# One attention + feed-forward block on one Trainium2 core: the feed-forward put into attention's hand order and buffers

## The chip, the cores and the metric

The kernel runs on one core of a Trainium2 chip. A core has five engines that run their own instruction streams and wait for one another by semaphores: PE (TensorE, matrix products and transposes into the PSUM memory), ACT (ScalarE), DVE (VectorE), POOL (GpSimd) and SP (SyncE, which here only issues transfers). PE's row is split in the profile into the matmuls (PE) and the loads of their stationary operand (PEld). The metric is the device time of one execution in microseconds. Before the change it is 5400.07 us, the median of 3 runs (5399.82 to 5401.36).

## What is computed

`x` is 8 x 1024 x 512 in float32 (B, S, E). The reference, cut to what matters:

```python
def attn(x):                      # H = 16 heads of HD = 32, q and k split into two halves
    q, k, v = split(x @ w_qkv)
    a = softmax(q1 k1 / sqrt(HD)) - lam * softmax(q2 k2 / sqrt(HD))
    out = a @ v
    out_n = out / sqrt(mean(out**2) + 1e-6) * norm_w * (1 - 0.8)
    return rearranged(out_n) @ wo

def ffn(x):                       # hidden 2048, rank 16
    h = bitlinear(x, w_fc) + gate * (x @ v.T @ fast_b.T @ u.T)
    r = maximum(h, 0)
    return bitlinear(r * r, w_proj)

x = x + attn(layernorm(x))
x = x + ffn(layernorm(x))
```

`bitlinear` multiplies by weights rounded to -1, 0 or 1 and by one scale for each output row.

## The kernel before

`block_kernel` runs two phases one after the other: `attention_phase` (lines 25 to 550) and `ffn_phase` (lines 778 to 969). What they share passes through the tensors `x1_dram[0]` to `x1_dram[15]` in DRAM: the rows after attention, in 16 groups of four tiles of 128 rows.

**Attention** works in 256 units: one head of one batch and one half of its queries, 32 units a batch. A unit takes the maxima of the scores (`max_scores`, L201, reduced by DVE at L208), makes the exponentials (`exp_scores`: PE at L254, ACT at L258), adds them up on POOL (`add_up`, L268 and L270) and multiplies by the values (`values`, through `quarters`, L275). `sums` adds the exponentials over the partitions with a matrix of ones (also L275). `heads_out` turns the result (L309) and divides (L319 to L332). After every fourth unit four steps follow: `rms_squares` (ACT, L343), `rms_sums` (DVE, L347), `rms_apply` (POOL, L353 to L356) and `output_rows`, which loads a tile of `x` (L365), multiplies by `wo` on PE (L368), adds (L375) and stores a tile to `x1_dram` (L376).

The order of PE, ACT, DVE and POOL is that in which the program names the instructions (`manual_schedule`); the order of SP's transfers is left to the compiler's scheduler. The loop (L485) makes the maxima two units ahead. The list `fill` holds the preparation of the next batch (layer norm, turning, values, projections: `prepare`), of which one step is taken at the head of a unit, at times also in its middle. In the last batch `fill` is empty, and the feed-forward weights are fetched instead (`prep.fetch`, L492): both halves of `wfc` and the first half of `wpr`. The second half of `wpr` takes the buffer of the last batch's values and is fetched after the loop (`prep.fetch_rest`, L543). Then `sums`, `heads_out` and the four steps of the last tile are written one after the other (L545 to L550), outside of the hand order.

**PSUM** has eight banks: three for `mx` (maxima), four for `one` (everything short) and one for `acc` (values). The feed-forward phase has four for `y`, two for `pf` and two for `tr` and `pt`.

**Feed-forward** takes the 16 groups of 512 tokens one after the other, each in 16 blocks of 128 hidden rows. `hidden(g, j)` makes eight matmuls (L885; tokens are split into a high and a low part, `hTh` and `hTl`) and one with the low-rank term (L888, operands `us` and `ts`); ACT takes the positive part (L890), POOL squares it (L892), DVE splits it into `r2h` and `r2l` (L895, L896). `contract` multiplies the block of two steps before by `wpr` into four banks (L902). At the group's end `output` scales (L913), adds `x` (L919) and stores (L922).

Between the blocks of group g the tokens of group g+1 are prepared: `load` in block 6 (L824, one transfer of 1 MB), `stats` in 7 and 8 (L833 to L838), `center` in 9 to 12 (L844, into `h`, two buffers), `turn` in 10 to 13 (L853 on PE into `tr`; L813 on ACT, L814 on DVE), `low_rank` in 14 (L865 with `m1`; L871 to L875 make `ts`). For group 0 all of it stands ahead of the first block, in the order of the scheduler:

```python
    load(0)
    for i in range(4):
        stats(0, i)
    for i in range(4):
        center(0, i)
        turn(0, i)
    low_rank(0)
```

Of the kernel before, what the change touches and what calls it, by code (L numbers as in the profile page):

```python
# [17 lines left out]
P = 128  # L18
# [6 lines left out]
def attention_phase(  # L25
    ctx, tc, consts, x, w_qkv, wo, lq1, lq2, lk1, lk2, norm_w, x1_dram, dpool, big, prep,
):

# [36 lines left out]
    wv = wpool.tile([P, KC, E], F32, name="wv")  # L65
# [46 lines left out]
    def norm_stats(b, t, xs=None):  # L112
        if xs is None:
            xs = p_x.tile([P, E], F32, tag="x", name="xs")
        nc.sync.dma_start(xs, x[b, t * P : (t + 1) * P])
# [165 lines left out]
    def values(u, kc):  # L281
        b, h = divmod(u // 2, H)
        if kc == 0:
            acc_of[u] = ps_acc.tile([P, HS // 2], F32, tag="acc", name="acc")
        quarters(
            acc_of[u], v_of[b][:, kc, h * HD : (h + 1) * HD], e_of[u, kc // 2][:, kc % 2],
            kc == 0, kc == NS - 1,
        )
# [71 lines left out]
    def output_rows(n):  # L360
# [5 lines left out]
        py = one_bank()  # L366
# [17 lines left out]
    def prepare(b):  # L384
        stats, tiles = {}, {}

        def start():
            begin_batch(b)
            stats[0] = norm_stats(b, 0)

        def advance(t):
# [3 lines left out]
            if t + 3 < NS:  # L395
                stats[t + 3] = norm_stats(b, t + 3)
# [28 lines left out]
    with tc.tile_pool(name="a_stage", bufs=1) as stage, tc.manual_schedule(engines=engines):  # L425
        begin_batch(0)
        xs4 = stage.tile([P, 4, E], F32, tag="tp", name="xs4", bufs=1)
        stats = [norm_stats(0, t, xs4[:, t - 4, :] if t >= 4 else None) for t in range(NS)]
# [44 lines left out]
    p_e = ctx.enter_context(tc.tile_pool(name="a_e", bufs=5))  # L473
    p_es = ctx.enter_context(tc.tile_pool(name="a_es", bufs=2))
    p_o = ctx.enter_context(tc.tile_pool(name="a_o", bufs=2))
    p_y = ctx.enter_context(tc.tile_pool(name="a_y", bufs=1))
    fill, later = [], {}
# [6 lines left out]
    with tc.manual_schedule(engines=engines):  # L484
        for s in range(0, NS * NU + 2, 2):  # L485
# [13 lines left out]
            if u < NU:  # L499
                if u % (2 * H) == 0 and kc == 0:  # L500
                    assert not fill
                    fill = prepare(u // (2 * H) + 1) if u + 2 * H < NU else []
# [40 lines left out]
    prep.fetch_rest()  # L543
    assert not later and list(adds.values()) == list(outs.values()) == [[NU - 1]]
    n = NU // 4 - 1  # L545
    for step in (
        lambda: sums(NU - 1), lambda: heads_out(NU - 1), lambda: rms_squares(n),
        lambda: rms_sums(n), lambda: rms_apply(n), lambda: output_rows(n),
    ):
        whole(step)  # L550
# [227 lines left out]
def ffn_phase(ctx, tc, consts, x1_dram, weights, out):  # L778

    nc = tc.nc
    B, S, E = out.shape
    HID, R = weights.HID, weights.R
    KC = E // P
    NJ = HID // P
    ident, neg_half = consts
    s_fc, s_pr = weights.s_fc, weights.s_pr  # L790


    p_o = ctx.enter_context(tc.tile_pool(name="f_o", bufs=6))
    late = ctx.enter_context(tc.tile_pool(name="f_late", bufs=1))
    early = ctx.enter_context(tc.tile_pool(name="f_early", bufs=1))
    ts = [p.tile([P, 512], F32R, name=f"ts{i}") for i, p in enumerate((early, late))]
    m1 = early.tile([P, KC, P], F32R, name="m1")
    us = early.tile([P, HID], F32R, name="us")
    p_s = ctx.enter_context(tc.tile_pool(name="f_s", bufs=2))
    p_h = ctx.enter_context(tc.tile_pool(name="f_h", bufs=2))  # L800
    nc.sync.dma_start(m1.bitcast(F32), weights.m1_d.rearrange("p k i r -> p k (i r)"))
    nc.sync.dma_start(us.bitcast(F32), weights.us_d)

    ps_y = ctx.enter_context(tc.tile_pool(name="f_ps_y", bufs=4, space=PSUM))
    ps_f = ctx.enter_context(tc.tile_pool(name="f_ps_f", bufs=2, space=PSUM))
    ps_t = ctx.enter_context(tc.tile_pool(name="f_ps_t", bufs=2, space=PSUM))

    p_hT = ctx.enter_context(tc.tile_pool(name="f_hT", bufs=2))
    p_r = ctx.enter_context(tc.tile_pool(name="f_r", bufs=3))

    def split(hi, lo, src):

# [209 lines left out]
```

## Time and profile before

| | us |
|---|---|
| median of 3 runs (lowest to highest) | 5400.07 (5399.82 to 5401.36) |
| the profiled execution | 5402.91 |
| its span, first to last instruction | 5401.1 |
| PE busy | 5293.1 |
| POOL busy | 4125.8 |
| DVE busy | 3791.5 |
| ACT busy | 2829.7 |
| first matmul of the feed-forward's low-rank product | at 4296.6 |

The page of a profile gives each engine's busy time and share. A table of stretches gives for each stretch of time its length, the busy time and number of instructions of each engine (PE, PEld, DVE, ACT, POOL), the granted clock of PE as a share of full speed, the busy share of the DMA engines and what they moved in GB/s. A line of the timeline begins with start and duration in us, then engine, line, operation, output and inputs; in brackets stands how long the engine had been idle before it and which instruction released it. "SPq" marks a transfer issued by SP; its duration is that of the issue. A line of the waits says who waited for whom: total us, how often, the longest.

### The profile page before, as it was taken

To read this page: it belongs to the slowest core of one execution; us is meant where nothing else is said; L and a number is where in the kernel's file an instruction comes from. 1 tells how busy PE (TensorE), PEld (TensorE's weight loads), DVE (VectorE), ACT (ScalarE), POOL (GpSimd) and SP (SyncE) were. 2 spreads that over 40 slices of the span, in tenths; PEclk is the share of its full clock that TensorE was granted. 3 is DMA by queue.
4 is the path that set the end of the run, shared out by engine and by line. 5 is a ranking of instruction groups with operands and counts; after the bars stand their busy time and mean duration, and the time that the engine had idled before them with its cause. 6 is when DMAs were issued, how large, how long until landed. Compare 5 with 4: busy or idle time off the path is not lost.

```text
span 5401.1 us, 105815 instructions
## 1 busy us (share of the span) xinstructions
PE 5293.1 (98%) x41522; PEld 3255.3 (60%) x41522; DVE 3791.5 (70%) x7539; ACT 2829.7 (52%) x5434; POOL 4125.8 (76%) x1501
## 2 busy tenths in 40 slices
PE   8999999999999999999999999999999899999999
PEld 4555555555555555555555555555555577777777
DVE  6877777787778777777787778777888445545554
ACT  4665666566656665665566556655666422222221
POOL 0998899889989998999899889988988633333333
PEclk9999999999999999999999999999999999999999
DMA  8112211211122112111211221122211101111111
GB/s 272 49 51 76 68 55 53 76 65 53 55 76 66 52 59 76 58 57 61 79 53 55 67 76 52 46 68 100 71 46 47 54 19 31 30 31 32 32 32 32
DMA packets 184865, 328.51 MB, mean 61 GB/s; under 512 B 32928, under 2 KB 55456, under 8 KB 183728
## 3 DMA queue, kind: packets, MB, share of 16 engines
q1 hardware_dynamic: 183440, 319.12, 18.5%
q8 instruction: 329, 5.39, 0.4%
q0 software_dynamic: 544, 2.10, 0.1%
q14 instruction: 168, 1.38, 0.1%
q10 hardware_dynamic: 384, 0.52, 0.0%
HBM read 209.16 MB, written 112.46 MB: 60 GB/s over the span
## 4 chain that ended last, share of the span: by engine, by line
PE 75%; POOL 10%; issue 8%; ACT 2%; DVE 2%; DMA 1%; SPq 0%; POOLq 0%; DVEq 0%; ACTq 0%
PE acc L275 17%; PE one L254 15%; PE mx L201 13%; PE one L154 8%; PE one L275 5%; PE one L368 4%; PE one L142 4%; POOL es L270 4%; PE y L902 3%; PE pf L885 3%; ACT e L258 2%; POOL r L892 2%; PE one L309 2%; POOL es L268 2%; POOL o L919 1%
## 5 line engine op out<-in xcount | busy, mean ns | idle before, releaser
L208 DVE TENSOR_REDUCE nm<-mx 128x1 f32<-128x512 f32 x4096 | 2549.4, 682 | 268.1 <-PE mx L201 263.6
L258 ACT ACTIVATE e<-one 128x512 f32<-128x512 f32 x4096 | 2116.9, 603 | 851.2 <-PE one L254 813.3
L270 POOL TENSOR_TENSOR es<-es,e 128x2048 f32<-128x2048 f32 x495 | 2262.4, 4570 | 66.2 <-ACT e L258 34.3
L268 POOL TENSOR_TENSOR es<-e 128x2048 f32<-128x2048 f32 x256 | 1170.0, 4570 | 287.3 <-ACT e L258 287.3
L275 PE MATMUL acc<-e,v 128*32 128x256 f32 x16384 | 1092.1, 384 | 0.0
L201 PE MATMUL mx<-tk,tq 64*128 64x512 f32 x4096 | 1055.8, 469 | 3.0 <-DVE nm L208 2.0
L201 PEld LDWEIGHTS mx<-tk,tq 64*128 64x128 f32 x4096 | 567.1, 183 | 539.8 <-DVE nm L208 303.0
L254 PE MATMUL one<-nms,one 64*128 64x512 f32 x4096 | 831.4, 394 | 8.0 <-ACT e L258 7.5
L254 PE MATMUL one<-tq,tk 64*128 64x512 f32 x4096 | 828.6, 391 | 0.0
L892 POOL TENSOR_TENSOR r<-r 128x512 f32<-128x512 f32 x256 | 270.1, 1058 | 652.8 <-ACT r L890 641.5
L275 PEld LDWEIGHTS acc<-e,v 128*32 128x32 f32 x16384 | 451.5, 109 | 432.0 <-issue 168.8
L890 ACT ACTIVATE r<-pf,s_fc 128x512 f32<-128x512 f32 x256 | 176.5, 690 | 811.0 <-PE pf L888 811.0
L895 DVE CAST r2h<-r 128x512 fp32r<-128x512 f32 x256 | 185.4, 724 | 456.7 <-POOL r L892 454.3
L154 PE MATMUL one<-hT,wqk 128*128 128x512 f32 x1024 | 472.8, 604 | 0.4 <-ACT e L258 0.4
L254 PEld LDWEIGHTS one<-nms,one 64*128 64x128 f32 x4096 | 413.5, 185 | 71.1 <-ACT e L258 15.5
L254 PEld LDWEIGHTS one<-tq,tk 64*128 64x128 f32 x4096 | 396.0, 184 | 82.1
L902 PE MATMUL y<-wpr,r2h 128*128 128x512 f32 x1024 | 415.1, 405 | 0.3
L902 PE MATMUL y<-wpr,r2l 128*128 128x512 f32 x1024 | 403.6, 394 | 0.3 <-DVE r2l L896 0.3
L885 PE MATMUL pf<-hTh,wfc 128*128 128x512 f32 x1024 | 403.5, 394 | 0.0
L885 PE MATMUL pf<-hTl,wfc 128*128 128x512 f32 x1024 | 403.3, 394 | 0.0
L162 DVE SCALAR_TENSOR_TENSOR pc<-one,pc 128x512 fp32r<-128x512 f32 x128 | 88.5, 691 | 345.1 <-ACT pc L161 345.0
L154 PEld LDWEIGHTS one<-hT,wqk 128*128 128x128 f32 x1024 | 184.1, 189 | 214.8 <-issue 186.4
(127 smaller groups left out, 4681.6 us busy)
## 6 DMA issues: line engine op xcount, KB each, us to landing
qk<-pc SPq DMA_DIRECT2D x128, 512.0 KB
tk<-qk SPq DMA_DIRECT2D x256, 256.0 KB
tq<-qk SPq DMA_DIRECT2D x512, 128.0 KB
xs<-in_L_attn_x SPq DMA_DIRECT2D x64, 256.0 KB
xr<-in_L_attn_x SPq DMA_DIRECT2D x256, 64.0 KB
x_dram<-y SPq DMA_DIRECT2D x64, 256.0 KB
xs<-x_dram SPq DMA_DIRECT2D x16, 1024.0 KB
out<-o SPq DMA_DIRECT2D x248, 64.0 KB
```

The source lines that it names most:

```text
L142: nc.tensor.matmul(pv, hT_of[b][:, kc, c * P : (c + 1) * P], wv[:, kc, :], start=(kc == 0), stop=(kc == KC - 1),)
L154: nc.tensor.matmul(ps, wqk[:, kc, c0 : c0 + P], hT_of[b][:, kc, tok], start=(kc == 0), stop=(kc == KC - 1),)
L201: nc.tensor.matmul(mx[sm], tq_of[u][rows, c * P : (c + 1) * P], tk_of[u // 2][rows, kh * 512 : kh * 512 + 512], start=True, stop=True,)
L208: nc.vector.tensor_reduce(nm_of[u][:, kh, sm, c : c + 1], mx[sm], AX.X, ALU.max, negate=True)
L254: nc.tensor.matmul(st[sm], w[rows, cols], m[rows, :], start=(w is one2), stop=(w is not one2))
L258: nc.scalar.activation(e[:, kc % 2, sm, :], st[sm], AF.Exp)
L268: nc.gpsimd.tensor_add(es_of[u], e_of[u, 0], e)
L270: nc.gpsimd.tensor_add(es_of[u], es_of[u], e)
L275: nc.tensor.matmul(out[32 * g : 32 * g + 32, :], w, e[:, g // 2, (g % 2) * (HS // 2) : (g % 2 + 1) * (HS // 2)], start=start, stop=stop,)
L885: nc.tensor.matmul(pf, w[:, kc, :], hT[:, kc, :], start=(kc == 0 and i == 0), stop=False)
L892: nc.gpsimd.tensor_mul(r2, r, r)
L902: nc.tensor.matmul(ys[i], r2[:, i * P : (i + 1) * P], weights.wpr[j // (NJ // 2)][:, j % (NJ // 2), :], start=(j == 0 and k == 0), stop=(j ...
```

## The change

Both phases become one function, `block_phases`, with the hand order over all of it from the attention loop on. In its parts:

- While the last batch runs, `fill` holds six steps of `prepare_tokens`: the four tiles of token group 0 are loaded, normed, turned and split. They take buffers of attention that are free by then (`pc`, `wv`, `x`).
- The pools of the exponentials (`a_e`, `a_es`) close after the loop, with `fetch_rest` and the last `sums` inside. Pools of the feed-forward (`us`, `m1`, `ts`, then tokens and outputs) open in their place; `m1` and `us` are loaded there.
- The last tile's `heads_out`, `rms_squares`, `rms_sums`, `rms_apply` and `output_rows` are written into blocks 0, 1, 2, 3 and 5 of group 0, with `low_rank(0)` ahead of block 0.
- The feed-forward uses attention's PSUM banks and buffers: `pf` in the three `mx` banks, `y` in the four `one` banks, `tr` and `pt` in the single `acc` bank; the squared values in `tq` and `tk`, tokens of even groups in `x`, `pc` and `wv`. The square is made in place.
- `h` has one buffer instead of two. The split of a turned tile is two instructions on ACT and two on DVE instead of one and one. Even groups are loaded by four transfers of 256 KB.
- `center`, `turn` and `low_rank` come one block later (10 to 13, 11 to 14, 15).

The diff, cut to its core:

```diff
+    p_h = ctx.enter_context(tc.tile_pool(name="a_h", bufs=1))
+    def begin_tokens(g):
+        if g % 2 == 0:
+            his = [p_pc.tile([P, 2, HS], F32R, tag="pc", name="hTh") for _ in range(2)]
+            lo = wpool.tile([P, KC, 512], F32R, tag="wv", name="hTl")
+        else:
+            hi = f_x.tile([P, KC, 512], F32R, tag="hTh", name="hTh")
+            his = [hi[:, 0:2], hi[:, 2:4]]
+            lo = f_x.tile([P, KC, 512], F32R, tag="hTl", name="hTl")
...
+    def split_turned(parts, i, tr):
+        his, lo = parts
+        cols = slice(i * P, (i + 1) * P)
+        for k in range(2):
+            nc.scalar.copy(his[k][:, :, cols], tr[:, 2 * k : 2 * k + 2, :])
+        for k in range(2):
+            nc.vector.tensor_sub(
+                lo[:, 2 * k : 2 * k + 2, cols], tr[:, 2 * k : 2 * k + 2, :],
+                his[k][:, :, cols].bitcast(F32),
+            )
...
+    def prepare_tokens():
+        stats, hs, parts = {}, {}, []
+        def apply(i):
+            xs, nb, rs = stats.pop(i)
+            hs[i] = p_h.tile([P, E], F32, tag="h", name="h")
+            nc.scalar.activation(hs[i], xs, AF.Identity, bias=nb, scale=rs)
+        def step(i):
+            if i == -2:
+                parts.append(begin_tokens(0))
+                x_of[0] = []
+            post = None
+            if i >= 0:
+                tr = one_bank().rearrange("p (k t) -> p k t", k=KC)
+                turn_h(hs.pop(i), tr)
+                post = lambda: (split_turned(parts[0], i, tr), apply(i + 1) if i + 1 < 4 else None)
+            if i + 2 < 4:
+                stats[i + 2] = norm_stats(x1_dram[0][i + 2])
+                x_of[0].append(stats[i + 2][0])
+            if i == -1:
+                apply(0)
+            return post
+        return [(lambda i=i: step(i), False) for i in range(-2, 4)]
...
-    with tc.manual_schedule(engines=engines):
+    ctx.enter_context(tc.manual_schedule(engines=engines))
+    with tc.tile_pool(name="a_e", bufs=5) as p_e, tc.tile_pool(name="a_es", bufs=2) as p_es:
...
-                    fill = prepare(u // (2 * H) + 1) if u + 2 * H < NU else []
+                    fill = prepare(u // (2 * H) + 1) if u + 2 * H < NU else prepare_tokens()
...
-    prep.fetch_rest()
+        prep.fetch_rest()
+        whole(lambda: sums(NU - 1))
...
+    f_w = ctx.enter_context(tc.tile_pool(name="f_w", bufs=1))
+    us = f_w.tile([P, HID], F32R, name="us")
+    m1 = f_w.tile([P, KC, P], F32R, name="m1")
+    ts = [f_w.tile([P, 512], F32R, name=f"ts{i}") for i in range(2)]
+    f_x = ctx.enter_context(tc.tile_pool(name="f_x", bufs=1))
+    nc.sync.dma_start(m1.bitcast(F32), prep.m1_d.rearrange("p k i r -> p k (i r)"))
+    nc.sync.dma_start(us.bitcast(F32), prep.us_d)
...
+    def load(g):
+        if g % 2:
+            xs = f_x.tile([P, 4, E], F32, tag="x", name="xs")
+            nc.sync.dma_start(xs, x1_dram[g].rearrange("n p e -> p n e"))
+            x_of[g] = [xs[:, i, :] for i in range(4)]
+        else:
+            x_of[g] = [p_x.tile([P, E], F32, tag="x", name="xs") for _ in range(4)]
+            for i in range(4):
+                nc.sync.dma_start(x_of[g][i], x1_dram[g][i])
...
+    def work_bank():
+        return ps_acc.tile([P, 512], F32, tag="acc", name="wb")
+    def turn(g, i):
+        tr = work_bank().rearrange("p (k t) -> p k t", k=KC)
+        turn_h(h_of.pop((g, i)), tr)
+        split_turned(parts_of[g], i, tr)
...
+        r = p_tq.tile([P, HS], F32R, tag="tq", name="r").bitcast(F32)
+        nc.scalar.activation(r, pf, AF.Relu, scale=s_fc[:, j : j + 1])
+        nc.gpsimd.tensor_mul(r, r, r)
+        r2 = p_tk.tile([P, S], F32R, tag="tk", name="r2")
+        r2h, r2l = r2[:, 0:512], r2[:, 512:1024]
...
     n = NU // 4 - 1
-    for step in (
-        lambda: sums(NU - 1), lambda: heads_out(NU - 1), lambda: rms_squares(n),
-        lambda: rms_sums(n), lambda: rms_apply(n), lambda: output_rows(n),
-    ):
-        whole(step)
+    rest = {
+        0: lambda: heads_out(NU - 1), 1: lambda: rms_squares(n), 2: lambda: rms_sums(n),
+        3: lambda: rms_apply(n),
+        5: lambda: output_rows(n, lambda: ps_mx.tile([P, 512], F32, tag="mx", name="py")),
+    }
+    low_rank(0)
...
-                if g + 1 < NG and 9 <= j < 13:
-                    center(g + 1, j - 9)
-                r2_of[k] = hidden(g, j)
+            if g + 1 < NG and 10 <= j < 14:
+                center(g + 1, j - 10)
+            r2_of[k] = hidden(g, j)
+            if ends:
+                ends.pop(0)()
+            if k in rest:
+                whole(rest.pop(k))
-                if g + 1 < NG and 10 <= j < 14:
-                    turn(g + 1, j - 10)
-                if g + 1 < NG and j == 14:
-                    low_rank(g + 1)
+            if g + 1 < NG and 11 <= j < 15:
+                turn(g + 1, j - 11)
+            if g + 1 < NG and j == 15:
+                low_rank(g + 1)
```

## The prediction

> **What bounds the kernel now.** I read the page first, then a table of stretches, then the timeline of the hand-over from attention to feed-forward, then the waits of the feed-forward stage.
>
> ```profile
> PE 5293.1 (98%) x41522; PEld 3255.3 (60%) x41522; DVE 3791.5 (70%) x7539; ACT 2829.7 (52%) x5434; POOL 4125.8 (76%) x1501
> ```
>
> TensorE (PE) is busy 98% of the span, so only its idle time, its slow-clock time and the work it is given can change the end. The stretches (length, busy time of each engine, PE clock, DMA share, GB/s) show where idle time is:
>
> ```profile
> 4118.00:4177.00 59.00, 56.65 (x576) 33.69 (x572) 47.69 (x99) 37.26 (x75) 49.88 (x14) 1.00 0.16 47
> ...
> 4272.15:4280.20 8.05, 0.74 (x4) 0.26 (x3) 1.82 (x6) 1.00 (x2) 4.16 (x3) 0.76 1.02 387
> 4280.20:4285.40 5.20, 5.15 (x8) 2.06 (x8) 0.01 (x1) 0.00 (x0) 0.00 (x0) 0.72 1.03 373
> ...
> 4291.10:4303.80 12.70, 9.69 (x32) 7.08 (x32) 5.40 (x9) 3.98 (x7) 0.00 (x0) 0.64 0.00 0
> ...
> 4310.00:5390.00 1080.00, 1066.07 (x4665) 849.73 (x4663) 534.59 (x836) 229.22 (x358) 360.10 (x344) 1.00 0.10 29
> ```
>
> The last attention batch (first row, four units) is nearly full. From 4272.15 to 4303.8 PE mostly waits and, when it works, has 0.64 to 0.76 of its clock. The feed-forward stage loses 13.9 us in 1080. The hand-over itself:
>
> ```profile
> 4270.19 0.42 SPq L801 DMA_DIRECT2D m<-m_d  x1
> ...
> 4270.71 1.80 SPq L762 DMA_DIRECT2D wpr<-wpr_d  x4
> ...
> 4276.11 2.91 POOL L354 TENSOR_TENSOR ss<-ss,neg_half 128x16 f32<-128x16 f32 x1
> 4279.10 1.05 POOL L356 TENSOR_TENSOR og<-og,ss 128x512 f32<-128x512 f32 x1
> ...
> 4285.40 0.75 DVE L375 SCALAR_TENSOR_TENSOR y<-one,nw,xr 128x512 f32<-128x512 f32 x1 [9.66 <-PE one L368]
> ...
> 4300.23 0.40 PE L865 MATMUL pt<-hTl,m 128*128 128x512 f32 x1
> ...
> 4303.84 0.50 PE L888 MATMUL pf<-ts,us 128*128 128x512 f32 x1 [1.58 <-DVE ts L875]
> ```
>
> It is one chain: head sums end at 4272.15, then the last head is turned, normed on POOL, multiplied by wo, added and only then is token group 0 centred, turned, taken through low_rank, until the first block's closing matmul (L888) at 4303.84. That is **31.7 us**. In the feed-forward stage two lines of the waits (total, times, longest) carry the idle time:
>
> ```profile
> DVE bs L833 <- DMA xs<-x_dram: 54.0, 14, 5.1
> ...
> PE tr L853 <- DVE h L844: 13.6, 13, 2.8
> ```
>
> The load at block 6 lands late, DVE's statistics and centring come late, and 13 times PE arrives at the turn of block 10 before the centred tile.
>
> **The change, part by part**, against the profiled execution (span 5401.1).
>
> *1. Hand-over.* After the head sums PE goes straight to low_rank(0), whose tokens were turned in the last batch. It needs m1. The new pool f_w opens after a_e and a_es close and takes their memory, so I expect m1 and us to be issued only when the last reader, the head sums, ends (4272.15). The four wpr loads, released when the last values end, are emitted before and will be ahead: 4270.71 to 4272.51 in the old row. At the 387 GB/s of the second row, full from about 4272, 2.10 MB of wpr and 0.26 MB of m1 need 6.1 us: m1 is there at 4278.1. PE has then been idle 5.9 us; after the old idle time its matmuls came every 0.43 us instead of 0.23 (rows at 4297 to 4300). Eight at 0.43: the last starts at 4281.1. From that start to L888 the old row needs 3.61 us (4300.23 to 4303.84: ACT and DVE splitting pt). L888 at 4284.7, 12.6 us after the sums instead of 31.7: **-19.1**. Bounds: m1 early, full clock, 7 x 0.23 + 3.61 = 5.3 us, -26.4; us (1.05 MB, 2.7 us) ahead of m1 too, -16.4. I take the middle one, since the emission order speaks for it.
>
> *2. Rows moved beside the blocks.* The last heads_out is 4 transposes (0.66, at 4268.70), output_rows 8 matmuls (3.67 at full clock, at 4201.00). PE has no room beside the blocks: **+4.3**. The rest is hidden. On POOL rms_apply (0.20 + 2.91 + 1.05 = 4.2) delays one squaring by about 1.4 us, and a block's r2 has some 5 us until contract two blocks later; ACT's squares and DVE's head work (1.3) sit in engines half idle. Its four xr loads stay early on SP, its store is needed by group 15 alone. Without that cover PE would wait for og as it does now, 7.2 us.
>
> *3. Group 0 in the last batch.* Four turns. A turn costs PE 0.45 us (4.37 us from turn to turn against 3.93 without), 1.8 in all, in a stage where PE has 2.4 of 59 idle. POOL gets 1.0 us a tile (0.19, 0.55 and 0.27: the same three small instructions of the earlier batches), ACT 0.83 to apply and two copies of 0.37 (the 128x256 copy of L301), DVE 0.68 + 0.18 and two subtractions. The steps fall at 3785 to 3855, where POOL is busy 14.8 of 15 and PE 13.1 to 14.8. The four token loads go through SP, which has time, into buffers free since the last preparation. Between 0 (all in PE's gaps) and 8 (PE 1.8, POOL 4, some ACT delay on top) I take **+2.5**.
>
> *4. Turns a block later.* Centring in blocks 10 to 13, turns in 11 to 14, low_rank in 15. The lateness, at most 2.8, is less than one block (3.93), so the 13.6 goes. Two stretches of 68 us had a clock of 0.97, about 2 us each, with the longest of these waits; I count 3 of the 4. **-16.6** (bounds -13.6 and -17.6). What is late next is the low-rank result: from low_rank's last matmul (4498.26) to its last DVE write (4502.01) 3.75 us; PE now has contract and eight matmuls between, 17 x 0.23 = 3.93. That holds by 0.2; up to 0.3 x 15 = 4.5 if not.
>
> *5. Single buffers.* tr and pt share one PSUM bank, h has one buffer. So a centring waits for the turn before it, at the head of DVE, with r2h, r2l and the split behind it; and a turn waits for the split before it. A block of the old kernel with a turn:
>
> ```profile
> 4483.52 0.60 PE L853 MATMUL tr<-ident,h 128*128 128x128 f32 x4
> ...
> 4484.55 1.04 POOL L892 TENSOR_TENSOR r<-r 128x512 f32<-128x512 f32 x1 [3.55 <-ACT r L890]
> ...
> 4485.62 0.43 DVE L895 CAST r2h<-r 128x512 fp32r<-128x512 f32 x1 [2.15 <-POOL r L892]
> ...
> 4486.15 0.69 DVE L896 TENSOR_TENSOR r2l<-r,r2h 128x512 fp32r<-128x512 f32 x1
> ...
> 4486.77 0.68 DVE L814 TENSOR_TENSOR hTl<-tr,hTh 128x512 fp32r<-128x512 f32 x1
> ```
>
> Centring (0.54) can run from 4484.2 to 4484.7, while DVE would wait for POOL anyway. The split is now two halves of about 0.43 (between 0.30 for 128 and 0.69 for 512 columns), done at about 4487.55; the next turn is due at 4487.90. It holds by 0.3 us. Sixty bank hand-overs (15 x 3 turns and 15 low_rank) give 0 to 12 (0.2 each); I take **+3**. Shorter instruction halves cost ACT and DVE 0.15 each, hidden.
>
> *6. Loads of even groups* come as four of 256 KB instead of one of 1 MB. The weights moved as 512 KB pieces one behind the other at 369 to 428 GB/s, and the load has a block more of time: 0.
>
> The Trainium skill speaks against that: "DMA: Bandwidth & Descriptors", section Rules for kernel authors, asks for 1 MiB or more in a DMA. Its table (1 MB 78% of peak, 64 KB 32%) would make a 256 KB piece perhaps half as fast, an estimate of some 2 us more per even load; by that the sum stays the same, since the later turn covers it, and no row here shows 256 KB loads in a queue.
>
> **Sum**: -19.1 + 4.3 + 2.5 - 16.6 + 3 = **-25.9**. The span becomes 5375.2. The profiled execution took 5402.91, 1.8 more than its span, and stands 2.84 above the median of 5400.07; against the median it is **5374.2 us**.
>
> **Rivals.**
> - *m1 is there in time* (SP order, or early release). For it: in the old order m1 stands before wpr. Against it: the memory of a_e is read until 4272.15. -26.4 in place of -19.1: 5367.
> - *The single bank holds PE a little*, 0.3 us on each of 60 hand-overs: 18 in place of 3, 5389. For it: a margin of 0.3 in which any added semaphore time counts. Against it: DVE's own rows fit. Half of this lies within 0.2% of before, which is about what a measurement of this kernel can tell from no change.
> - *The rows are not covered*: the change doesn't do that part; PE meets L368 in order before og is ready and waits up to 7.2: 5381. Against it: og has five blocks.
> - *Slower*: the loop turn, centring, r2, split, turn gets longer than a block. Place: DVE in blocks 11 to 15. DVE's cast r2h takes 1.50 us in place of 0.43 where it meets POOL (the row at 4460.90, beside an output add). If centring and the squaring now meet in the same way, every loop gains 1.07, less 0.3 of margin: 0.8 x 60 = 48 in place of 3, 5419. It decides for slower from 0.6 us a hand-over ((25.9 - 3 + 10.8) / 60). Against it: in turn blocks POOL has no output add, and centring would start 0.4 before POOL does.
>
> **Numbers.** Forecast 0.50, m1 in time 0.17, rows not covered 0.05, bank a little 0.18, slower 0.10. Range: the low end takes m1 in time with no bank wait and free turns (about 5361), the high end the upper bounds of parts 3 and 5 together or the bank rival (5391); it leaves out the slower rival and the upper half of the bank rival. Faster by over 0.2%: 0.50 + 0.17 + 0.05 + 0.09 = 0.81; same 0.09; slower 0.10.
>
> **What would show it.** Part 1: PE's gap after the head sums, its releaser a DMA of m, 5 to 6 us long, clock near 0.5 after it; L888 some 12 to 13 us after the sums. Part 2: no wait on og, L368 inside the blocks. Part 3: units 226 to 229 longer by under a microsecond each. Part 4: the wait of the turn for h gone. Part 5: waits of PE on DVE for hTl or of DVE for the turn, below 0.2 us. A gap in front of L888 of every group, or a turn block of more than 4.5 us, would make the prediction wrong.

## The result, and the profile after

The changed kernel takes **5361.31 us** (median of 6 runs, 5358.5 to 5366.5); the kernel before, on the same chip, 5401.67 (6 runs, 5399.82 to 5403.63). The ratio is 0.9927, 95% interval 0.9916 to 0.9937. The forecast was 5374.2 us, a gain of 25.9. The gain is about 40, and 5361.31 lies at the lower edge of the range (5361 to 5391). So the sign was right, and a third of the gain is not in the sum.

The profiled execution took 5362.87 us, its span is 5360.9. PE is as full as before, and its busy time is shorter:

```profile
PE 5272.0 (98%) x41522; PEld 3257.7 (61%) x41522; DVE 3788.1 (71%) x7599; ACT 2832.6 (53%) x5502; POOL 4126.8 (77%) x1511
```

The count of matmuls is the same, 41522, and PE's busy time is 21 us shorter (5293.1 before). The table of stretches (length, busy time and count of PE, PEld, DVE, ACT, POOL, clock, DMA share, GB/s), for the last batch, the gap of the hand-over, the work behind it, and the feed-forward stage:

```profile
4118.00:4177.00 59.00, 56.88 (x576) 33.83 (x572) 47.78 (x100) 37.23 (x74) 50.01 (x14) 1.00 0.16 47
4279.00:4285.90 6.90, 0.18 (x4) 0.00 (x0) 0.00 (x0) 0.37 (x1) 0.00 (x0) 0.68 1.00 397
4285.90:4293.00 7.10, 6.68 (x17) 4.99 (x17) 1.38 (x2) 1.63 (x3) 0.00 (x0) 0.59 0.61 232
4293.00:5350.00 1057.00, 1055.35 (x4702) 854.97 (x4702) 537.57 (x908) 233.26 (x422) 366.40 (x349) 1.00 0.11 30
```

One gap is left, in which the DMA engines are full, and a slow clock behind it; the feed-forward stage idles 1.7 us in 1057 where it idled 13.9 in 1080. The hand-over in the timeline:

```profile
4277.51 1.77 SPq L986 DMA_DIRECT2D wpr<-wpr_d  x4
...
4278.13 1.05 PE L278 MATMUL one<-e,ones 128*32 128x256 f32 x16
...
4279.44 0.58 SPq L624 DMA_DIRECT2D m<-m_d  x1
4280.07 0.45 SPq L625 DMA_DIRECT2D us<-us_d  x1
...
4285.94 0.77 PE L674 MATMUL wb<-hTh,m 128*128 128x512 f32 x1 [6.77 <-DMA m<-m_d]
4286.51 0.63 PE L674 MATMUL wb<-hTl,m 128*128 128x512 f32 x1
...
4292.90 0.50 PE L693 MATMUL pf<-ts,us 128*128 128x512 f32 x1 [0.38 <-DVE ts L682]
```

`m1` (the trace calls it m) stands behind the four `wpr` loads on SP. It is issued at 4279.44, when the head sums (L278) have just ended (4279.2), and PE begins with it 6.5 us later. Then the matmuls come every 0.43 us. The first closing matmul (L693, before L888) starts 13.7 us after the sums, where it was 31.7. (Counted from 4279.0, as some expectations below do, these are 13.9 us and a gap of 6.9.)

The waits of the feed-forward stage that answer to the two shown of before (waiter, releaser, total us, times, longest), PE's and then DVE's:

```profile
PE y L706 <- DVE r L700: 0.7, 3, 0.2
PE y L706 <- DVE r L699: 0.5, 1, 0.5
PE pf L693 <- DVE ts L682: 0.4, 1, 0.4
```

```profile
DVE h L654 <- PE wb L511: 48.7, 45, 1.3
DVE bs L645 <- DMA xs<-x_dram: 27.5, 7, 4.7
```

The turn no longer waits for the centred tile. The single buffer `h` does make DVE wait 45 times, for 48.7 us, and PE never feels it. DVE still waits for tokens, but 7 times instead of 14: only the odd groups, whose load is one transfer, are left.

Where the 40.2 us between the two spans lie (read from the same marks in both traces: the store of the maxima at the beginning and end of the last batch, the start of ACT's copy that follows the head sums, the first and the last closing matmul; us):

| stretch | before | after | difference |
|---|---|---|---|
| up to the last batch | 3781.71 | 3783.66 | +1.95 |
| last batch | 456.55 | 461.50 | +4.95 |
| to the end of the head sums | 33.89 | 34.08 | +0.19 |
| hand-over, to the first closing matmul | 31.69 | 13.66 | -18.03 |
| first to last closing matmul | 1083.85 | 1054.76 | -29.1 |
| tail | 13.44 | 13.29 | -0.15 |

The fifth row is the surprise. The waits that went and their clock are worth 13 to 17 us, and the rows of the last tile, now inside, should take 4 of them back. So I timed single blocks there: from closing matmul to closing matmul, mean of blocks 4 to 8 of groups 1 to 14, where nothing but `hidden` and `contract` is on PE. Before it is **3.933 us**, after **3.853**. For 256 blocks that would be 20 us, but a block with a turn became only 0.04 shorter (4.374 to 4.333). Counted over all blocks of the two traces, the fifth row splits like this ("lost" is the length of a block less that of an undisturbed block of its kind):

| part of the -29.1 | us |
|---|---|
| lost in block 10 of groups 0 to 14, to waits and slow clock: 19.4 before, 3.7 after | -15.7 |
| the rows of the last tile, in group 0 | about +4.0 |
| all blocks shorter | about -17.4 |

The hidden matmuls of such a block, in the timeline, before:

```profile
4562.51 0.39 PE L885 MATMUL pf<-hTh,wfc 128*128 128x512 f32 x1
4562.74 0.39 PE L885 MATMUL pf<-hTl,wfc 128*128 128x512 f32 x1
4562.98 0.39 PE L885 MATMUL pf<-hTh,wfc 128*128 128x512 f32 x1
4563.21 0.39 PE L885 MATMUL pf<-hTl,wfc 128*128 128x512 f32 x1
```

and after:

```profile
4563.27 0.39 PE L692 MATMUL pf<-hTh,wfc 128*128 128x512 f32 x1
4563.49 0.39 PE L692 MATMUL pf<-hTl,wfc 128*128 128x512 f32 x1
4563.72 0.39 PE L692 MATMUL pf<-hTh,wfc 128*128 128x512 f32 x1
4563.95 0.39 PE L692 MATMUL pf<-hTl,wfc 128*128 128x512 f32 x1
```

The durations are equal (0.39); it is the starts that lie 0.233 us apart before and 0.227 after. The clock is 1.00 in both, and nobody is waited for.

### The profile page after: what moved, and what is told of

It is laid out like the page before. It is cut to its first block, busy times and chain, and to the rows that moved or that the text cites. A ratio compares the mean times of both kernels' runs of the same rounds, so it can differ in the third digit from the quotient of the medians.

```text
span 5360.9 us, 105615 instructions
## 1 busy us (share of the span) xinstructions
PE 5272.0 (98%) x41522; PEld 3257.7 (61%) x41522; DVE 3788.1 (71%) x7599; ACT 2832.6 (53%) x5502; POOL 4126.8 (77%) x1511
## 4 chain that ended last, share of the span: by engine, by line
PE 84%; POOL 6%; issue 3%; ACT 3%; DVE 1%; DMA 1%; SPq 0%; POOLq 0%; ACTq 0%; DVEq 0%
PE acc L278 17%; PE one L257 16%; PE mx L204 13%; PE one L157 8%; PE y L706 6%; PE pf L692 6%; PE one L278 5%; PE one L145 4%; PE one L371 4%; POOL es L273 3%; ACT e L261 2%; PE one L312 2%; POOL es L271 1%; POOL r L696 1%; PE pf L693 1%
## 5 line engine op out<-in xcount | busy, mean ns | idle before, releaser
L278 PE MATMUL acc<-e,v 128*32 128x256 f32 x16384 | 1093.8, 384 | 0.0
L278 PEld LDWEIGHTS acc<-e,v 128*32 128x32 f32 x16384 | 453.2, 110 | 431.7 <-issue 170.1
L706 PE MATMUL y<-wpr,r 128*128 128x512 f32 x2048 | 524.2, 397 | 2.0 <-DVE r L700 0.9
L699 DVE CAST r<-r 128x512 fp32r<-128x512 f32 x256 | 179.7, 702 | 421.8 <-POOL r L696 421.7
L706 PEld LDWEIGHTS y<-wpr,r 128*128 128x128 f32 x2048 | 375.2, 188 | 97.2 <-DVE o L716 20.1
```

Source lines behind the costliest of these rows:

```text
L278: nc.tensor.matmul(out[32 * g : 32 * g + 32, :], w, e[:, g // 2, (g % 2) * (HS // 2) : (g % 2 + 1) * (HS // 2)], start=start, stop=stop,)
L706: nc.tensor.matmul(ys[i], r2[:, i * P : (i + 1) * P], prep.wpr[j // (NJ // 2)][:, j % (NJ // 2), :], start=(j == 0 and k == 0), stop=(j == ...
```

## The experiments

My theory for the hand-over, the rows and the later turns stood as predicted. For the shorter block there were four candidates: the later turn (fewer waits of some kind), the square in place, the number or the numbers of PSUM banks, and the place of the operands in SBUF, which the new buffers moved. The allocator had put the turned h and the relu tiles of the kernel before at multiples of 1024 bytes in each SBUF row; in the changed kernel they start 64 above a multiple (even groups, and the relu tiles) or 576 above one (odd groups). The weights are 832 above one in both.

### Part 4 alone: the turns a block later

The kernel before, with one edit:

```diff
-                if g + 1 < NG and 9 <= j < 13:
-                    center(g + 1, j - 9)
+                if g + 1 < NG and 10 <= j < 14:
+                    center(g + 1, j - 10)
...
-                if g + 1 < NG and 10 <= j < 14:
-                    turn(g + 1, j - 10)
-                if g + 1 < NG and j == 14:
+                if g + 1 < NG and 11 <= j < 15:
+                    turn(g + 1, j - 11)
+                if g + 1 < NG and j == 15:
```

> The kernel before with one thing of the change alone: centring in blocks 10 to 13, turning in 11 to 14, low_rank in 15. If PE's waits for the centred tile are what this part removes, 13.6 us of waiting and some clock after the longest waits go: 5384 to 5388, with the plain block (closing matmul to closing matmul) still 3.93 us. If the later turn is also what shortened the plain block from 3.93 to 3.85 us in the changed kernel, another 20 us go, about 5365.

Measured: 5389.52 us (10 runs) beside 5400.48, ratio 0.9977 (0.9968 to 0.9987). From first to last closing matmul 13.0 us less; the plain block stays 3.933. In the stretch from 4293 the waits of the turn for h were 13.6 us in 13; now the view has one line for them:

```profile
PE tr L853 <- DVE h L844: 5.8, 1, 5.8
```

This one wait belongs to group 0, which is turned ahead of the first block (at 4293.86; before the change at 4291.13, outside of the stretch). Between the blocks no wait for h is left. Block 10 still loses 6.6 us over its groups, where it was 19.4. Of these 4.1 are in group 7, where PE waits for r2h and r2l (0.9 and 1.1 us) and has half its clock from 4818.44 to 4821.85. So the step is right, its size is 11 us in the median and 13.0 in the trace where 16.6 were predicted, and the shorter block has another cause.

### The square in place, and the PSUM banks

Two kernels before with one part of the change each. The first squares in place and splits into one tile of two halves:

```diff
-        r = p_r.tile([P, 512], F32, tag="r", name="r")
+        r = p_r.tile([P, 512], F32R, tag="r", name="r", bufs=5).bitcast(F32)
...
-        nc.gpsimd.tensor_mul(r2, r, r)
...
+        nc.gpsimd.tensor_mul(r, r, r)
+        r2 = p_r.tile([P, S], F32R, tag="r2", name="r2")
+        r2h, r2l = r2[:, 0:512], r2[:, 512:1024]
```

> The kernel before with only the squaring made in place and the two parts of the square in one tile, as in the change. If this sets the spacing of the matmuls (fewer buffers, one release instead of two for each block), the plain block falls from 3.93 to 3.85 us and the time by about 20 us, to 5381. If PSUM banks, the order or the places in SBUF do it, block and time stay: 3.93 us, 5400.

The second gives three banks to `pf` and one to `tr` and `pt`:

```diff
-    ps_f = ctx.enter_context(tc.tile_pool(name="f_ps_f", bufs=2, space=PSUM))
-    ps_t = ctx.enter_context(tc.tile_pool(name="f_ps_t", bufs=2, space=PSUM))
+    ps_f = ctx.enter_context(tc.tile_pool(name="f_ps_f", bufs=3, space=PSUM))
+    ps_t = ctx.enter_context(tc.tile_pool(name="f_ps_t", bufs=1, space=PSUM))
```

> The kernel before with three PSUM banks for the hidden block and one for turns and low rank instead of two and two, as in the change. If the bank division sets the spacing of the matmuls, the plain block falls to 3.85 us and the time to about 5381. If not, 3.93 us and 5400; a single bank for turns alone should cost nothing, or a few tenths of a us for each turn at most.

Measured: 5397.34 us, ratio 0.9995 (0.9986 to 1.0004), and 5398.14 us, 0.9996 (0.9986 to 1.0005). The plain block is 3.933 in both. Neither is the cause. The second also answers the rival of the single bank: a block with a turn takes 4.375 us with one bank and 4.374 with two.

A third kernel keeps the counts and exchanges the numbers of the banks, by opening the pool of `pf` ahead of that of `y`:

```diff
+    ps_f = ctx.enter_context(tc.tile_pool(name="f_ps_f", bufs=2, space=PSUM))
     ps_y = ctx.enter_context(tc.tile_pool(name="f_ps_y", bufs=4, space=PSUM))
-    ps_f = ctx.enter_context(tc.tile_pool(name="f_ps_f", bufs=2, space=PSUM))
```

> The kernel before with the pool of the hidden sums opened ahead of the pool of the output sums, so that hidden sums lie in PSUM banks 0 and 1 and output sums in 2 to 5, in place of 4, 5 and 0 to 3; sizes and order of work as before. Theory of the banks: the plain block falls from 3.933 us to about 3.85, ratio 0.996. Rivals, place in SBUF or order of instructions: 3.933 us, ratio 1.000.

Measured: 5396.53 us, ratio 0.9996 (0.9987 to 1.0006), plain block 3.933. The numbers of the banks are not the cause either.

### The place of the operands in SBUF

The kernel before, with a tile of 64 bytes that is written once and never read, ahead of the pools of h, of the turned h and of the relu tiles:

```diff
+    shift = ctx.enter_context(tc.tile_pool(name="f_shift", bufs=1)).tile([P, 16], F32, name="shift")
+    nc.gpsimd.memset(shift, 0.0)
```

> The kernel before with a 64-byte tile ahead of the feed-forward's pools, so that h's turned halves, the relu tiles and their halves start 64 bytes further in each SBUF row, as the even blocks' do in the changed kernel; nothing else differs. Theory of the place in the row: a plain block (closing matmul to closing matmul) falls from 3.933 us to 3.85, 256 blocks give 20 us, ratio 0.996. Rival, banks of PSUM or the order of instructions: the block stays 3.933 us, ratio 1.000.

Measured: the plain block is **3.854 us**, the value of the changed kernel, in all groups. A stretch of the timeline of this kernel:

```profile
4562.19 0.39 PE L887 MATMUL pf<-hTl,wfc 128*128 128x512 f32 x1
4562.42 0.39 PE L887 MATMUL pf<-hTh,wfc 128*128 128x512 f32 x1
4562.65 0.39 PE L887 MATMUL pf<-hTl,wfc 128*128 128x512 f32 x1
```

The instructions are those of the kernel before, and the starts are now 0.227 us apart. From first to last closing matmul it takes 1064.74 us in place of 1083.85, 19.1 less. The time is 5390.41 us (10 runs, 5384.32 to 5394.85) beside 5398.66, ratio 0.9983 (0.9974 to 0.9992): faster by 8, not by 19. The two traces are not typical. That of the kernel before (5402.91) is 4.2 above this median of 27, that of the shifted one (5384.32) is the fastest of its ten. Of the 19.1, the shorter blocks are 16.7; the other 2.4 are block 10, which loses 16.9 here and 19.4 there. This loss differs from execution to execution: in the four traces with unchanged blocks and early turns (before, and the last three experiments) it is 19.4, 17.9, 10.3 and 14.5 us. The four slowest of the ten executions have a mean clock of 0.996, the others 0.997. I take it that the shorter blocks give part of their gain back in such waits and their clock; no trace of a slower execution shows it, so it stays open.

The same theory, undone in the changed kernel: 448 bytes ahead of the odd groups' tiles, 576 behind them. That puts their turned h at a multiple of 1024 and leaves PE's other operands where they were, so the even groups of the same execution are the control.

```diff
+    def gap(n, name):
+        t = ctx.enter_context(tc.tile_pool(name=name, bufs=1)).tile([P, n // 4], F32, name=name)
+        nc.gpsimd.memset(t, 0.0)
+    gap(448, "f_gap0")
     f_x = ctx.enter_context(tc.tile_pool(name="f_x", bufs=1))
+    gap(576, "f_gap1")
```

> The changed kernel with 448 bytes put ahead of the odd groups' tiles (tokens and turned h), and 576 behind them, so that the odd groups' turned h starts at a multiple of 1024 bytes in each SBUF row, as all of it does in the kernel before, while the even groups' stays where it was (64 above a multiple). Theory of the place: in odd groups the hidden matmuls go back to 0.233 us and a plain block to about 3.91 us (8 x 0.0067 more), in even groups it stays 3.853; 8 x 16 x 0.055 = 7 us, time some 5368 us, ratio to before 0.994. Rival, something else in the changed kernel makes its blocks short: 3.853 in both, 5361 us.

Measured: plain block 3.926 in odd groups, 3.853 in even ones, without one exception in the 70 blocks measured (3.926 to 3.927, and 3.853 to 3.854). In an odd group the starts are 0.233 us apart again:

```profile
4399.92 0.39 PE L698 MATMUL pf<-hTh,wfc 128*128 128x512 f32 x1
4400.15 0.39 PE L698 MATMUL pf<-hTl,wfc 128*128 128x512 f32 x1
4400.39 0.39 PE L698 MATMUL pf<-hTh,wfc 128*128 128x512 f32 x1
4400.62 0.39 PE L698 MATMUL pf<-hTl,wfc 128*128 128x512 f32 x1
```

The time is 5369.15 us, 7.8 above the changed kernel's (ratio to before 0.9947, 0.9930 to 0.9963; the changed kernel's is 0.9927, 0.9916 to 0.9937, so the times alone would not settle it). The blocks do: the place is the cause of their length, shown in both directions.

What about the place counts? Three more kernels before, each with other places. In the first the turned h lies some 45 KB lower, 832 above a multiple of 1024, and the relu tiles stay:

```diff
+    p_hT = ctx.enter_context(tc.tile_pool(name="f_hT", bufs=2))
     p_o = ctx.enter_context(tc.tile_pool(name="f_o", bufs=6))
...
-    p_hT = ctx.enter_context(tc.tile_pool(name="f_hT", bufs=2))
```

> The kernel before with the pool of h's turned halves opened first in the feed-forward, so that they lie some 45 KB lower in each SBUF row, and the small tiles (us, ts) move up instead; relu's tiles and halves stay where they are. Theory that the moving operand's place in the row sets the spacing of the hidden matmuls: their spacing changes from 0.233 us towards 0.227, that of contract (0.230) does not, the plain block is about 3.88 us, ratio 0.998. Rivals, banks or order of instructions: 3.933 us, ratio 1.000.

In the other two gaps of chosen sizes stand between the pools, so that even and odd groups differ (here the second; the third has 64 bytes ahead of the first pool, 64 between and 896 behind):

```diff
-    p_hT = ctx.enter_context(tc.tile_pool(name="f_hT", bufs=2))
+    p_hT = [ctx.enter_context(tc.tile_pool(name="f_hT0", bufs=1))]
+    gap(512, "f_gap1")
+    p_hT.append(ctx.enter_context(tc.tile_pool(name="f_hT1", bufs=1)))
+    gap(576, "f_gap2")
```

> The kernel before with the relu tiles and their halves 64 bytes above a multiple of 1024, h's turned halves of even groups left at a multiple of 1024, those of odd groups at a multiple of 512 that is none of 1024. If each operand counts by itself, contract falls to 0.2267 us in all groups, hidden stays 0.233 in even groups and a plain block is 3.90 there. If only multiples of 1024 are slow, odd groups are at 3.853; if multiples of 512 are too, they equal the even ones. If the relu tiles alone were the cause, all are at 3.853.

> The kernel before with h's turned halves of even groups 64 bytes above a multiple of 1024, those of odd groups 128 above one, and the relu tiles left at a multiple of 1024. If each operand counts by itself, hidden falls to 0.2267 us in even groups, contract stays at 0.2303 and a plain block is 3.88 to 3.89. If a shift of 128 bytes is as good as one of 64, odd groups equal the even ones; if not, they stay at 3.933.

All blocks measured, by the place of the turned h and of the relu tiles (bytes above a multiple of 1024):

| turned h | relu tiles | plain block, us | kernel |
|---|---|---|---|
| 0 | 0 | 3.933 | before |
| 0 | 64 | 3.926 | even groups of the second; odd groups of the undone one |
| 512 | 64 | 3.927 | odd groups of the second |
| 128 | 0 | 3.922 | odd groups of the third |
| 64 | 0 | 3.893 | even groups of the third |
| 832 | 0 | 3.894 | the first |
| 64 | 64 | 3.854 | before, shifted; even groups after |
| 576 | 64 | 3.853 | odd groups after |

The first of the three took 5391.38 us, ratio 0.9990 (0.9981 to 0.9999); the other two have one time each (5398.9 and 5397.2) and stand here for their blocks alone. Three places of h are good (64, 576, 832), two are bad (0, 512), and 128 is nearly as bad. That fits odd multiples of 64, though these six places don't prove it. My expectation that each operand counts by itself fell: moving h alone gives 0.040, the relu tiles alone 0.007, both 0.079. And in the second kernel the spacing of contract, which reads the moved relu tiles, is 0.2292 us on the mean, not the 0.2267 that I expected. In the first, moving h alone shortened the spacing of contract too (0.2299 to 0.2285), and that of hidden only half of the way (0.2327 to 0.2294). What in SBUF or in PE's reading makes this difference isn't settled by these runs.

### The hand-over: m1 ahead of half of the weights

The changed kernel with `fetch_rest` behind the loads of `m1` and `us`. The scheduler then puts two of the four `wpr` loads ahead of `m1` and two behind `us`.

```diff
-        prep.fetch_rest()
...
     nc.sync.dma_start(us.bitcast(F32), prep.us_d)
+    prep.fetch_rest()
```

> The changed kernel with the second half of wpr named after m1 and us, so that two of its four loads instead of all four stand ahead of m1 on SP. If the bytes ahead of m1 set PE's gap after the last head sums (6.9 us now), 1 MB less at about 390 GB/s shortens the gap by 2.7 us to about 4.2 and the time by 2.5 to 4 us (some clock too), 5358. If the gap is a fixed latency of the load or of the release of the exponentials' memory, it stays at 6.9 us, and so does the time.

Measured: 5361.39 us (ratio to before 0.9926, 0.9912 to 0.9941), no different from the changed kernel. PE's gap shrinks from 6.8 to 5.7 us, the closing matmul comes 12.6 us after the sums, 1.0 less and not 2.7. PE begins with `m1` 5.6 us after its issue, with half of the weights in front of it. In the 5.73 us of the gap the DMA engines moved 379 GB/s, some 2.2 MB, where these weights and `m1` are 1.3. So what is queued behind `m1` took its share of them too.

### The last batch

I thought that POOL cost the 5 us of the last batch: it adds without a gap at the place of the new steps, and each new tile puts 1.0 us of small instructions between. In the changed kernel PE waits there for the last of these adds:

```profile
3828.80 0.66 PE L204 MATMUL mx<-tk,tq 64*128 64x512 f32 x2
3832.17 1.07 PE L278 MATMUL one<-es,ones 128*32 128x256 f32 x16 [2.71 <-POOL es L273]
```

In the traced execution of the last experiment the same wait is 2.77 us, and behind it PE's clock is down:

```profile
3831.54 1.93 PE L278 MATMUL one<-es,ones 128*32 128x256 f32 x16 [2.77 <-POOL es L273]
```

1.93 us in place of 1.07 for the same 16 matmuls; that execution lost 9.3 us in its last batch. With the odd groups put back, the wait was 2.77 us as well, and the 16 matmuls took 1.07. So waits of one length stand with and without a slow clock behind them.

The granted clock of the traces changes on a grid. In the kernel before, it is 0.50 from 4409.46 to 4412.87 us and from 4617.67 to 4621.08. Both stretches are 3.41 us long, and they begin 208.21 us apart, 61 times 3.413. The Trainium skill, "TensorE: Matmul & The Clock Gate", Part 1, says that the clock gate watches activity over a window of about 3.4 us that is free-running. The grid agrees with that. That the place of a wait in the window decides about the clock behind it would fit these rows; it is not shown.

If POOL's backlog is what costs, the steps should stand behind it. The changed kernel with eight empty steps ahead:

```diff
-        return [(lambda i=i: step(i), False) for i in range(-2, 4)]
+        later_on = [(lambda: None, False)] * 8
+        return later_on + [(lambda i=i: step(i), False) for i in range(-2, 4)]
```

> The changed kernel with eight empty steps ahead of the preparation of group 0, which then begins about 20 us later in the last batch, behind the stretch in which GpSimd adds without a gap. If the 5 us that the last batch lost come from GpSimd's backlog there, they fall to about 2 us, and the time to some 5357 us (ratio to before 0.992); if they are PE's own turns, the time stays at 5361 us (0.993). If the steps now end too late for the first block, PE waits for hTl ahead of the first hidden matmul, some us, and the time rises.

Measured: 5361.05 us (ratio to before 0.9927, 0.9915 to 0.9940), the time of the changed kernel. In its trace, the fastest of its five executions (5355.25), the last batch costs 3.85 us instead of 4.95, with no slow clock. That speaks for the rival, PE's own turns. So I took the last batch as one stretch, in the kernel before, in the changed one and in this one (length, then PE's busy time and count):

```profile
3781.70:4238.30 456.60, 436.88 (x4395) 258.91 (x4391) 368.11 (x761) 287.29 (x566) 392.93 (x104) 1.00 0.16 50
```

```profile
3783.70:4245.20 461.50, 441.63 (x4411) 261.46 (x4407) 373.58 (x777) 292.23 (x578) 396.96 (x116) 1.00 0.16 50
```

```profile
3780.80:4241.20 460.40, 440.09 (x4411) 260.10 (x4407) 373.64 (x777) 292.32 (x578) 397.05 (x116) 1.00 0.15 49
```

PE's idle time is 19.7 us before, 19.9 after and 20.3 with later steps: its gaps took up nothing. What grows is its busy time, by 3.2 us for 16 transposes without a slow clock (0.8 a turn), and by 4.75 in the changed kernel, which between 3840 and 3860 has a clock of 0.91. The waits for POOL's adds are 2.9 us in all before and 3.0 after, though the longest grew from 1.7 to 2.7. My theory that the backlog takes the 5 us fell; whether the one longer wait brings on the slow clock isn't settled.

### What the runs point to, put together

The changed kernel with the later steps, with `m1` of the first group loaded some units earlier into a free slot of the queries' ring (the permanent copy follows behind `us`), `us` ahead of half of the weights, and the odd groups' tokens loaded in four pieces:

```diff
-        prep.fetch_rest()
+        m1_0 = p_tq.tile([P, HS], F32R, tag="tq", name="m1").rearrange("p (k r) -> p k r", k=KC)
+        nc.sync.dma_start(m1_0.bitcast(F32), prep.m1_d.rearrange("p k i r -> p k (i r)"))
...
-    nc.sync.dma_start(m1.bitcast(F32), prep.m1_d.rearrange("p k i r -> p k (i r)"))
     nc.sync.dma_start(us.bitcast(F32), prep.us_d)
+    prep.fetch_rest()
+    nc.sync.dma_start(m1.bitcast(F32), prep.m1_d.rearrange("p k i r -> p k (i r)"))
...
-            nc.sync.dma_start(xs, x1_dram[g].rearrange("n p e -> p n e"))
             x_of[g] = [xs[:, i, :] for i in range(4)]
+            for i in range(4):
+                nc.sync.dma_start(x_of[g][i], x1_dram[g][i])
...
-                nc.tensor.matmul(pt, m1[:, kc, :], hT, start=(n == 0), stop=(n == 2 * KC - 1))
+                nc.tensor.matmul(pt, (m1 if g else m1_0)[:, kc, :], hT, start=(n == 0), stop=(n == 2 * KC - 1))
```

> The changed kernel with what the runs point to: the preparation of group 0 begins eight units later, the first group's m1 is loaded some units earlier into a free slot of the queries' ring, the odd groups' tokens are loaded in four pieces like the even ones'. If m1 is what the hand-over waits for, PE's gap behind the head sums (6.9 us) goes, the first closing matmul comes 6 us after the sums in place of 13.9, limited by the low-rank path (3.8 us behind its matmuls); us may hold it some us more. The last batch costs 4 in place of 5. If the single 1 MB load makes block 10 of even groups long, that block falls to 3.86 and gives 3 to 4 us. Sum some -12: 5349 us, ratio to before 0.9905. If us is the next that is late, 5355 us.

Measured: **5354.37 us** (5351.03 to 5355.7) beside 5399.25, ratio 0.9918 (0.9904 to 0.9933), the lowest median of all kernels here. The hand-over:

```profile
4277.43 0.82 SPq L990 DMA_DIRECT2D wpr<-wpr_d  x2
...
4279.03 0.50 PE L678 MATMUL wb<-hTh,m 128*128 128x512 f32 x1
...
4279.27 0.32 SPq L626 DMA_DIRECT2D us<-us_d  x1
4279.64 0.91 SPq L990 DMA_DIRECT2D wpr<-wpr_d  x2
...
4282.56 0.39 PE L696 MATMUL pf<-hTl,wfc 128*128 128x512 f32 x1
4286.26 0.47 PE L697 MATMUL pf<-ts,us 128*128 128x512 f32 x1 [3.31 <-DMA us<-us_d]
```

PE goes from the sums to the low-rank product without a gap. The wait has moved one operand on: `us` is issued when the memory of the exponentials is free, and PE, which waits 3.3 us for it, can begin 7.0 us after that. The closing matmul comes 7.1 us after the sums instead of 13.7. This is the second of the two cases expected (5355 us, `us` late). The load in four pieces did its part: block 10 is 3.85 us in all 15 groups, where the changed kernel had 3.85 to 5.19 in the even ones. The last batch missed what was expected of it: it costs 6.8 us in this execution, not 4, with half the clock from 3935.77 to 3939.18 and from 3966.49 to 3969.90.

## Why the prediction was right or wrong

| step | predicted | measured | from |
|---|---|---|---|
| 1 hand-over | -19.1 | -18.0 | the two traces |
| 2 rows moved | +4.3 | about +4.0 | blocks 0 to 5 of group 0; `output_rows` is 3.43 of it, no wait for og |
| 3 group 0 in the last batch | +2.5 | +5.0 | the two traces |
| 4 turns a block later | -16.6 | -15.7 | block 10 in the two traces; -12.8 in that of part 4 alone |
| 5 single buffers | +3 | 0 | 4.375 against 4.374 |
| 6 loads of even groups | 0 | no loss | even groups are prepared without a wait for tokens |
| place of the operands | no term | -17.4 | all blocks of the two traces; -16.7 in that of the shift alone |

The measured terms sum to -42.1. They are cut from one trace of each kernel, so they add up by construction: the spans differ by -40.2, or by -42.2 without the +1.95 that lies ahead of the last batch. The +1.95 is scatter: five executions of the changed kernel and its variants stand there between -0.9 and +3.0. Block 10 scatters more (10.3 to 19.4 us lost with early turns), so the -15.7 holds for these two executions.

- **The step that failed is the block itself.** Parts 4 and 5 took the 3.93 us of a block over from the old trace, as if eight plus one plus eight matmuls at full clock had one length. The change moved their operands in SBUF, and the block became 0.08 us shorter, some 17 us in all. The prediction had no term for it, and its list of what would prove it wrong looked at turns and gaps only, not at a plain block.
- **That 5361.31 lies in the range is luck.** The low end, 5361, stood for `m1` in time, free turns and no wait for the bank. `m1` was late and the turns cost twice their term; the time came down there by the term that was missing.
- **Part 1 held with its mechanism**: `m1` behind four `wpr` loads, the gap, the slow clock, 13.7 us where 12.6 were predicted. PE begins with `m1` 6.7 us after the sums, and not 5.9, and needs 0.3 more from there to the closing matmul. The rival "m1 in time" (-26.4) describes a kernel that had to be built: with `m1` early the closing matmul comes 7.1 us after the sums, and not 5.3, because `us` is late.
- **Part 2 held.** `output_rows` stands inside the blocks without a wait in front, on the chain of the changed kernel:

```profile
4309.51 3.43 PE py L371 x8
```

- **Part 3 was half of what it is.** A turn was priced at 0.45 us, as beside full blocks of the feed-forward, and a part of it was to vanish in PE's gaps. In the last batch a turn takes 0.8 us of PE and no gap takes any of it; a stretch of slow clock adds 1 to 2 us in this execution. The sign named for it failed too: not every unit is longer by under a microsecond, since two of the distances between the stores of the maxima grew by 2.0 and 1.7. The 4 us for POOL that the upper bound held didn't come. The bounds (0 to 8) held the sum.
- **Part 4 held**, within 0.9 us in these two traces. What it didn't foresee is that tokens of odd groups (one load of 1 MB) stay late: block 10 of the group before, which is 3.85 us when undisturbed, takes up to 5.19 there, 3.6 us more in sum over eight groups. Low-rank, which I had within 0.2 us of being late, was not.
- **Part 5 and its rivals cost nothing.** DVE waits 48.7 us for the single `h`, in time that it had; neither the single bank (4.375) nor the loop turn, centring, squaring, split showed in PE's time. A turn block of the changed kernel takes 4.333 us, 0.48 more than a plain one, where it was 0.44 more; the shifted kernel, which keeps two buffers and two banks, has the same 0.48 (4.335), so they aren't what adds it.
- **Part 6**: four pieces were better than one load, and not merely as good; the 2 us more per even load that were estimated beside the sum did not show. I take it that the statistics of the first tile begin when its piece is there. DVE waited 4.7 us at the longest for the 1 MB load, and 1.7 in the last kernel, where all came in pieces:

```profile
DVE bs L649 <- DMA xs<-x_dram: 7.5, 7, 1.7
```

- **Slips that change nothing in the forecast.** The slower rival decides from 0.66 us a hand-over, since its 3 is to be added and not taken off; 7 x 0.23 + 3.61 is 5.2; the upper bounds of parts 3 and 5 give 5389, not 5391. And 256 KB loads did stand in the old profile (64 of x and 256 of tk), though none of them was timed there.

## What to carry to other kernels

A change that moves buffers is also a change of every operand's address: compare the spacing of equal matmuls before and after, not only waits and gaps, and when it differs without a wait or a clock, shift the tiles by 64 bytes and look again. A hand-over ends with the operand that lands last; after moving one load forward, price the next one in the queue, since the wait moves there. Work put into a stage whose PE is 96% busy cost its own time there: the small gaps that are left between waits took none of it. And a term read from one pair of traces can be off by several microseconds: time lost to waits in block 10 was 10.3 to 19.4 us in four executions with the same blocks.

## What the runs showed of the hardware

- With matmuls of 128 x 128 by 512 columns in this kernel's float32 form, the spacing at full clock is 0.227 us or 0.233 us, depending on where in the SBUF row the operands start: a gain of 2% of the block for 64 bytes. Starts at 64, 576 and 832 above a multiple of 1024 were fast, at 0 and 512 slow, at 128 nearly as slow. Both operands moved together (0.079 us a block) gave more than the sum of each alone (0.040 and 0.007).
- A wait of 2.77 us at the same place of the program left the 16 matmuls behind it at 1.07 us in one execution and stood before 1.93 in another. The granted clock is halved for stretches of 3.41 us or a multiple of it.
- PE could begin with a load of 256 KB 6.5 us after its issue when 2 MB stood before it on the same queue, and after 5.6 us with 1 MB before it and 2 MB following.
